# Last product of the output projection: token tiles in the order 0, 2, 1, 3, and the gate multiplied ahead

## The chip, the core and the metric

The kernel runs on one core of a Trainium2 chip. The time is device microseconds of the core, the median over runs. The engines have queues of their own and wait for one another through semaphores: TensorE (PE in the profile; PEld is its weight load), VectorE (DVE), ScalarE (ACT), GpSimd (POOL) and SyncE (SP), which issues nearly all DMAs.

## What is computed

A layer of lightning attention with a routed gate, on x of 4 sequences, 512 tokens each and 512 features, all in float32:

```python
xn = layernorm(x)
s = lightning_attn(xn)        # 16 heads of 128, blocks with decay
g = silu(router_ffn(xn))      # top 8 of 64 experts
out = x + s * g
```

The attention ends in `s = (gate * norm_w * o * rms) @ w_out.T`, where `rms` is one number per token over all 2048 features of `o`. Since it is one number per token, the kernel applies it behind the output projection, together with `g`.

## The kernel before

**Stages.** V projection, then for each pair of sequences (p = 0, 1) the gate, q and k projections with the attention of each head, and at the end the output projection with the router's sum and the final `x + s * g`. Matrix products run as three passes over operands split into a high and a low part (PASSES, lines 27 and 1234): ScalarE writes the high part (line 110), VectorE or GpSimd the low one (line 113).

**Output projection.** For each pair p the product of two sequences with two column halves is made by seven products in place of eight (OUT_PRODUCTS, line 49). Product m runs over 8 groups g of two heads; so there are 112 steps (p, m, g), in the loop of line 1244. A step is 4 token tiles x 3 passes = 12 matmuls of 128x256 (`o_group`, line 1232). Tiles 0 and 1 add up in the two halves of one PSUM accumulator, tiles 2 and 3 in those of another (`acc[t // 2][:, t % 2]`).

**Operands.** `yr` is the left operand of two steps: a load on SP (`load_y`), a cast on ScalarE and a subtraction on VectorE (`split_y`, 128x1024), written into the program five steps ahead (`ahead`, line 1109). Three buffers of it are in use here, so a cast waits until TensorE has done the pair of steps before. `wr` is the right operand of a product, two halves of it, each one cast and two VectorE subtractions of 128x512 (`split_wo`, line 860), written at g = 2 and g = 5 of the product before. Call yr51 the one of steps 102 and 103 (g = 6, 7 of the last pair's sixth product), yr52 to yr55 those of the seventh product's pairs of steps.

**Sums.** After each product `o_sums` (line 890) combines its accumulator with earlier ones that stay in SBUF (`a`, `e`, `c`), and from the fourth product on gives one quarter of the output to `finish` (line 876). For a 128x256 piece that is: VectorE `u = src * rms * u` (L879), where `u` held the gate; GpSimd `u = u + x` (L880); a store from `u`. The stores are issued on SP when the loop comes to g = 3 of the next product (line 1258). In the profile e_o, c_o and a_o are the pieces of the fifth, sixth and seventh product. The second accumulator's sums are written one step into the next product.

**The tail.** In the very last product the last three groups are not run group by group, but tile by tile (TAIL, lines 1287 to 1293): tile t gets its nine matmuls, and then its sums: VectorE `a = acc + a` (L900), `u = a * rms * u` (L879), `u = u + x` (L880, here on VectorE too), and a store, of even tiles on SP and odd ones on ACT (L882).

**Order.** The program's order is each queue's order: the loop writes a step's operands first, then its matmuls, then sums, and nothing is reordered. Every engine takes its instructions in that order.

**Memory.** `decay_row`, 1 KB on each of 16 partitions, holds a table of decays. It is made at the start, and its last reader is a store early in the V projection (`keep_rows`). It lives in the pool of constants, for the whole program. `stage` is a pool that is closed at the end of the V projection; `late` is the pool of the output projection.

Of the kernel before, what the change touches and what calls it, by code (L numbers as in the profile page):

```python
# [8 lines left out]
F32 = mybir.dt.float32  # L9
F32R = mybir.dt.float32r  # L10
AF = mybir.ActivationFunctionType
ALU = mybir.AluOpType
AX = mybir.AxisListType

P = 128
NH = 16
GH = 2
NG = NH // GH
PB = 2
# [41 lines left out]
def kernel(  # L61
# [13 lines left out]
    nc = tc.nc  # L75
# [5 lines left out]
    NT = N // P  # L81
# [6 lines left out]
    def pool(stack, name, bufs=1, **kw):  # L88
        return stack.enter_context(tc.tile_pool(name=name, bufs=bufs, **kw))


    def left(stack, name, bufs=1):
        return pool(stack, name, bufs, side="left", reuse_waits="tile")

    def right(stack, name, bufs=1):
        return pool(stack, name, bufs, side="right", reuse_waits="tile")

    const = pool(ctx, "const")
# [7 lines left out]
    def tok(b, t):  # L106
        return bass.ds(b * N + t * P, P)
# [13 lines left out]
    ones = const.tile([P, 1], F32, tag="ones", name="ones")  # L121
    mhalf = const.tile([P, NT], F32, tag="mhalf", name="mhalf")
    W = 2 * P
    decay_row = const.tile([NH, W], F32, tag="decay_row", name="decay_row")
    by_row = const.tile([P, 2], F32, tag="rest_of", name="rest_of")
    rest_of, slope_of = by_row[:, 0:1], by_row[0:NH, 1:2]
    kdecay = const.tile([P, NH], F32, tag="kdecay", name="kdecay")
# [19 lines left out]
    NM, NQ, H2 = len(PRODUCTS), NG // 2, F // 2  # L147
# [47 lines left out]
    rms = [const.tile([P, NT], F32, tag=f"rms{b}", name=f"rms{b}") for b in range(B)]  # L195
# [25 lines left out]
    def rsqrt(dst, var, scale, eps, name):  # L221
        n = dst.shape[1]
        v = small.tile([P, NT], F32, tag="var", name=f"v_{name}")
        nc.vector.tensor_scalar(v[:, 0:n], var, scale, eps, ALU.mult, ALU.add)
        nc.gpsimd.tensor_tensor(dst, v[:, 0:n], mhalf[:, 0:n], ALU.pow)

    xts = {}
# [328 lines left out]
    def nothing():  # L556
        return [[] for _ in PRODUCTS]
# [7 lines left out]
    def v_weights(p, g, rawp, sump, wp):  # L565
        def loads(raw):
            r = raw.rearrange("p i k (c w) -> p i k c w", c=KC)
            per = VH // GH
            return [
                (r[:, i, k, :, bass.ts(j, GH * P)], w_v[(2 * g + i) * per + j][:, bass.ts(k, KC)])  # L570
                for i in range(2) for k in range(2) for j in range(per)
            ]
        return Weights(f"v_{p}_{g}", KC * VW, rawp, sump, wp, loads, True)
# [209 lines left out]
    def sum_squares(b):  # L783
        ps = ps_sc.tile([P, NT], F32, tag="sc", name=f"ssq_{b}")
        for t in range(NT):
            nc.tensor.matmul(
                ps[:, t : t + 1], sq[b][:, bass.ts(t, P)], ones, start=True, stop=True
            )
        rsqrt(rms[b], ps, 1.0 / (NH * P), RMS_EPS, f"rms{b}")

    gates, ebs = {}, []

    def load_eb(outp):
        ebs.append(outp.tile([P, F], F32, tag="x", name="raw_eb", bufs=PB * NT))
        nc.sync.dma_start(out=ebs[0][0:E, :], in_=expert_b)
        nc.sync.dma_start(out=ebs[0][E : 2 * E, :], in_=expert_b)
# [78 lines left out]

    def finish(b, t, src, j, m, last):
        u, xt, c = gates[b, t], xts[b, t], bass.ts(j, H2)
        tail_ = last and m == NM - 1
        nc.vector.scalar_tensor_tensor(u[:, c], src, rms[b][:, t : t + 1], u[:, c], ALU.mult, ALU.mult)  # L879
        (nc.vector if tail_ else nc.gpsimd).tensor_tensor(u[:, c], u[:, c], xt[:, c], ALU.add)  # L880
        if tail_:
            (nc.scalar if t % 2 else nc.sync).dma_start(out=out[tok(b, t), c], in_=u[:, c])  # L882
        elif last or m > 4:
            d = c if last else slice(0, F)
            stores.append(lambda: nc.sync.dma_start(out=out[tok(b, t), d], in_=u[:, d]))

    ochain = {}


    def o_sums(p, m, x, ps, ts, last):  # L890
        b0 = p * PB
        name = f"o{m}{x}_{p}"

        def temp(n, pool_, tag, bufs=None):
            k = 4 if tag == "sum" else 2
            ochain[n, x] = pool_.tile([P, k, H2], F32, tag=tag, name=f"{n}_{name}", bufs=bufs)[:, 0:2]
            return ochain[n, x]

        def add(dst, what, i=slice(0, 2)):
            nc.vector.tensor_tensor(dst[:, i], ps[:, i], ochain[what, x][:, i], ALU.add)  # L900
        s1 = (wk, "s1", 1) if x == 0 else (late, "s1b", 1) if p or m else (hpools["sum"], "sum", None)
        if m == 0:
            nc.scalar.copy(temp("s1", *s1), ps)
        elif m == 1:
            add(temp("a", wk, "a", 2), "s1")
        elif m == 2:
            add(temp("e", wk, *(("e", 1) if x == 0 else ("sqs", 2))), "a")
        else:

            i2, j2 = ((0, 0), (1, 1), (0, 1), (1, 0))[m - 3]  # L910
            dst = (lambda: ps, lambda: ochain["e", x], lambda: temp("c", *s1), lambda: ochain["a", x])[m - 3]()
            if m > 3:
                add(dst, "e" if m == 4 else "a", slice(ts[0], ts[-1] + 1))
            for i in ts:
                finish(b0 + i2, 2 * x + i, dst[:, i], j2, m, last)
# [60 lines left out]
    stage = right(vs_stack, "stage", 4)  # L976
    rawp, sump = right(vs_stack, "vraw"), right(vs_stack, "vsum")
    vwp, vout = left(vw_stack, "vw", 8), left(vw_stack, "vout", 4)
    ws = [v_weights(0, g, rawp, sump, vwp) for g in range(NV)]
    tiles = [(p, t) for p in range(NP) for t in range(NT)]  # L980
    again = [(p, t) for p in reversed(range(NP)) for t in range(NT)]
# [50 lines left out]
    for k, (p, t) in enumerate(tiles + again):  # L1032
        g, after = k // n1, nothing()
# [106 lines left out]
    for i, (p, kind, n, w) in enumerate(todo):  # L1140
# [19 lines left out]
        if nu - len(XN) + NX <= i < nu:  # L1160
# [3 lines left out]
            m = i - (nu - len(XN) + NX)  # L1164
# [79 lines left out]
    for i, (p, m, g) in enumerate(steps):  # L1244
        last = p == NP - 1
        if i == 6:
            while ysums:
                ysums.pop(0)()

        if i == 16:  # L1250
            ha_stack.close()
            hw_stack.close()
            late = right(late_stack, "late", 2)

        ahead(i, 9 if i == 15 else 10, 5)
        if i == 16:
            load_eb(late)
        while stores and g == 3:
            stores.pop(0)()
        if g == 0:  # L1260
            k, first = OUT_PRODUCTS[m][2:]
            if m < 3:
                q, tag = (ps_sc, "sc") if k == 2 else (ps_mm, "mm")
                if k == 2:
                    spare[:] = [ps_sc.tile([P, F], F32, tag="sc", name=f"spare_{p}")]
                accs[k] = [q.tile([P, 2, H2], F32, tag=tag, name=f"acc{k}{x}_{p}") for x in range(2)]
            acc = accs[k]
        for j, f in ((2, 0), (5, 1)):
            u = i // NG + 1
            if g == j and u in made:  # L1270
                split_wo(made[u], f, win.pop(0))
                nxt = order.index((u, f)) + 2
                if nxt < len(order):
                    win.append(load_wo(made[order[nxt][0]], order[nxt][1]))
        if i == 17:
            split_eb(late)
        for b, t in tiles_at.get(i + 6, ()) if i > 16 else tiles_at[20]:
            if t == 0 and i >= 16:
                load_wT(b, late)

        for b, t in tiles_at[20] if i == 16 else tiles_at.get(i + 5, ()) if i > 16 else ():
            load_x(late, b, t, PB * NT)
        for d, step in ((3, silu_gate), (1, gate_sum), (-1, lambda b, t: center(b, t, late))):
            for b, t in tiles_at.get(i - d, ()):
                step(b, t)
        yr = parts.pop(0)
        if last and m == NM - 1 and g >= NG - TAIL:
            tail.append(yr)
            if g == NG - 1:
                for t in range(NT):  # L1290
                    for n in range(TAIL):
                        o_group(acc, m, NG - TAIL + n, tail[n], t)
                    o_sums(p, m, t // 2, acc[t // 2], (t % 2,), True)
        else:
            for t in range(NT):
                o_group(acc, m, g, yr, t)
            if g == NG - 1:
                for j in range(2):
                    sums.append(lambda p=p, m=m, j=j, a=acc[j], last=last: o_sums(p, m, j, a, (0, 1), last))
                sums.pop(0)()  # L1300

        if sums and (g == 0 or m < 2 or i + 1 < len(steps) and OUT_PRODUCTS[steps[i + 1][1]][2] == k):
            sums.pop(0)()
        if i in (1, 3, 5):
            for f in last_steps[i // 2]:
                f()
        if i in (8, 10):
            sum_squares((b0, b1)[i // 2 - 4])
        for b, t in tiles_at.get(i, ()):
            ffn(b, t)  # L1310
    late_stack.close()
# [44 lines left out]
```

## Time and profile before

| | |
|---|---|
| median of 3 runs | 1057.78 us (1057.56 to 1059.29) |
| profiled execution | 1057.22 us |
| its span, first to last instruction | 1055.4 us |
| matmuls of the output projection, L1235 | 1344, mean 282 ns |
| seventh product of the last pair, first matmul to last | about 1038 to 1051.2 us |

In the profile a line such as `1030.85 1.76 DVE L113 TENSOR_TENSOR yr<-yin,yr 128x1024 fp32r<-128x1024 f32 x1` reads: start and length in us, engine, line of the kernel, operation, what is written from what, the shape of one instruction, and how many stand together. Square brackets at the end hold the engine's idle time before it and what ended that. The waits have three numbers: us in total, how often, and the longest. The view of windows has the stretch, its length, busy time and number of instructions of each engine, and last the granted TensorE clock, the DMA share and GB/s.

### The profile page before, as it was taken

How to read it: one execution, taken by the hardware profiler on the slowest of the kernel's cores; microseconds unless marked ns; L12 is line 12 of the kernel's file. 1: busy time of each engine (PE TensorE's matmuls, PEld its weight loads, DVE VectorE, ACT ScalarE, POOL GpSimd, SP SyncE). 2: the span in 40 equal slices, each digit the busy share in tenths (PEclk: the TensorE clock that was granted, in tenths of full speed). 3: DMA queues.
4: the chain of work that ended last, by engine and by line, in shares of the span. 5: the costliest groups of instructions: out<-in, count | busy, mean ns of one | idle time of the engine just before them, and what ended most of it. 6: DMA issues, size and time to landing. Idle time of an engine off the chain costs nothing.

```text
span 1055.4 us, 17634 instructions
## 1 busy us (share of the span) xinstructions
PE 1042.5 (99%) x6338; PEld 924.5 (88%) x6338; DVE 637.3 (60%) x1017; ACT 553.4 (52%) x969; POOL 680.7 (64%) x698
## 2 busy tenths in 40 slices
PE   9999999999999999999999999999999999999997
PEld 7888888887888878888888888888888889999997
DVE  6666543357677676765554555545555558698767
ACT  5555555554545545455554555545545545574632
POOL 5888781857768776786777778877678753124013
PEclk9999999999999999999999999999999999999999
DMA  7456736544455454553863323533334236989863
GB/s 246 166 203 245 265 141 230 159 125 150 150 150 195 135 170 153 162 183 112 285 225 108 137 66 114 177 109 115 96 108 147 76 135 222 347 299 305 283 220 100
DMA packets 128839, 185.12 MB, mean 175 GB/s; under 512 B 11105, under 2 KB 72689, under 8 KB 127857
## 3 DMA queue, kind: packets, MB, share of 16 engines
q1 hardware_dynamic: 127856, 183.56, 52.7%
q8 instruction: 50, 0.82, 0.3%
q10 hardware_dynamic: 896, 0.44, 0.2%
q14 instruction: 37, 0.29, 0.1%
HBM read 115.26 MB, written 70.80 MB: 176 GB/s over the span
## 4 chain that ended last, share of the span: by engine, by line
PE 91%; DVE 4%; DMA 2%; ACT 1%; issue 1%; POOL 0%; SPq 0%; ACTq 0%; DVEq 0%
PE u_qk L516 27%; PE u_g L516 15%; PE u_v L516 13%; PE acc L1235 12%; PE sa L672 5%; PE o L757 5%; PE ss L695 4%; PE o L759 4%; PE d_v L546 2%; DMA yin<-y 2%; PE kt L675 2%; PE lg L332 1%; PE pt L265 1%; DVE yS L720 1%; DVE wosum L746 1%
## 5 line engine op out<-in xcount | busy, mean ns | idle before, releaser
L1235 PE MATMUL acc<-wr,yr 128*128 128x256 f32 x1344 | 163.4, 282 | 1.3 <-DVE a_o L900 1.3
L1235 PEld LDWEIGHTS acc<-wr,yr 128*128 128x128 f32 x1344 | 161.4, 190 | 3.3 <-DVE a_o L900 1.7
L516 PE MATMUL u_qk<-blk_T,ws_qk 128*128 128x512 f32 x576 | 141.7, 395 | 0.9 <-DVE best L380 0.9
L769 POOL TENSOR_TENSOR sqs<-sqs,sq 128x512 f32<-128x512 f32 x60 | 79.1, 1318 | 94.6 <-ACT sq L768 94.6
L516 PEld LDWEIGHTS u_qk<-blk_T,ws_qk 128*128 128x128 f32 x576 | 106.9, 188 | 23.9 <-issue 1.3
L113 POOL TENSOR_TENSOR ws_qk<-sum_qk,ws_qk 128x512 fp32r<-128x512 f32 x64 | 84.7, 1335 | 29.7 <-ACT ws_qk L110 29.7
L516 PE MATMUL u_qk<-blk_B,wa_qk 128*128 128x512 f32 x384 | 101.7, 400 | 0.0
L880 POOL TENSOR_TENSOR u<-u,x 128x256 f32<-128x256 f32 x28 | 32.4, 1179 | 100.5 <-DVE u L879 70.4
L113 DVE TENSOR_TENSOR yr<-yin,yr 128x1024 fp32r<-128x1024 f32 x56 | 75.3, 1349 | 34.9 <-ACT yr L110 34.8
L560 ACT ACTIVATE k<-k 128x512 f32<-128x512 f32 x64 | 40.5, 632 | 106.2 <-DVE k L507 106.2
L757 PE MATMUL o<-at,vin 128*128 128x128 f32 x512 | 88.5, 275 | 0.0
L110 ACT CAST yr<-yin 128x1024 fp32r<-128x1024 f32 x56 | 58.3, 1046 | 44.7 <-PE acc L1235 36.1
L516 PEld LDWEIGHTS u_qk<-blk_B,wa_qk 128*128 128x128 f32 x384 | 69.8, 189 | 13.6
L761 DVE SCALAR_TENSOR_TENSOR y<-o,nw,gt 128x512 f32<-128x512 f32 x64 | 48.0, 751 | 49.6 <-PE o L759 49.6
L757 PEld LDWEIGHTS o<-at,vin 128*128 128x128 f32 x512 | 74.8, 192 | 2.5
L681 ACT ACTIVATE kd<-kt,kdecay 128x384 f32<-128x384 f32 x64 | 37.2, 581 | 71.8 <-PE kt L675 71.8
L759 PE MATMUL o<-qd,st 128*128 128x128 f32 x384 | 74.3, 275 | 0.0
L768 ACT ACTIVATE sq<-o 128x512 f32<-128x512 f32 x60 | 35.9, 598 | 72.7 <-POOL sqs L769 41.7
L516 PE MATMUL u_g<-blk_T,ws_g 128*128 128x512 f32 x288 | 72.5, 396 | 0.0
L672 PE MATMUL sa<-q,k 128*128 128x128 f32 x512 | 68.0, 276 | 3.2 <-ACT q L560 3.1
L672 PEld LDWEIGHTS sa<-q,k 128*128 128x128 f32 x512 | 64.2, 191 | 7.3 <-ACT q L560 4.8
L699 DVE SCALAR_TENSOR_TENSOR st<-st,bdecay,ss 128x128 f32<-128x128 f32 x128 | 41.7, 346 | 44.2 <-ACT st L697 41.9
(199 smaller groups left out, 2402.3 us busy)
## 6 DMA issues: line engine op xcount, KB each, us to landing
yin<-y SPq DMA_DIRECT2D x56, 512.0 KB, 4.7
v<-vo_v SPq DMA_DIRECT2D x64, 256.0 KB, 2.8
raw_qk<-in_w_head_dram SPq DMA_DIRECT2D x64, 256.0 KB, 4.2
vin<-v SPq DMA_DIRECT2D x64, 256.0 KB, 3.5
y<-yS SPq DMA_DIRECT2D x64, 256.0 KB, 3.4
y<-y SPq DMA_DIRECT2D x48, 256.0 KB, 2.2
woin<-wo SPq DMA_DIRECT2D x18, 512.0 KB, 5.3
x<-in_x_dram SPq DMA_DIRECT2D x32, 256.0 KB, 4.9
```

The source lines that it names most:

```text
L110: nc.scalar.copy(hi, src)
L113: eng.tensor_tensor(lo, src, hi.bitcast(F32), ALU.subtract)
L516: nc.tensor.matmul(ps, lhsT, rhs, start=(first and c == 0 and n == 0), stop=(c == KC - 1 and n == len(PASSES) - 1), skip_group_check=not f ...
L560: nc.scalar.activation(dst, src, AF.Silu)
L672: nc.tensor.matmul(pa[:, c], k[:, c], q[:, c], start=True, stop=True)
L695: nc.tensor.matmul(ps[:, c], kd[s][:, c], v_of(b, h, c), start=True, stop=True)
L699: nc.vector.scalar_tensor_tensor(r[:, c], r[:, c - 1], bdecay[:, h : h + 1], ps[:, c], ALU.mult, ALU.add)
L757: nc.tensor.matmul(o, v_of(b, h, c), at[s][:, c], start=True, stop=(c == 0))
L759: nc.tensor.matmul(o, st[s][:, c - 1], qd[s][:, c - 1], start=False, stop=True)
L761: nc.vector.scalar_tensor_tensor(y, po, nw[:, h : h + 1], gts[s], ALU.mult, ALU.mult)
L769: nc.gpsimd.tensor_tensor(sq[b], sq[b], s1, ALU.add)
L1235: nc.tensor.matmul(acc[t // 2][:, t % 2], yr[:, yi, bass.ts(t, P)], wos[m, g // NQ][:, wi, g % NQ], start=(first and g == 0 and n == 0 and ...
```

## The change

- The tail takes the token tiles in the order 0, 2, 1, 3.
- The last product's piece is out = x + (acc + a) * rms * gate. The part that does not need the last accumulator is made during the sixth product, one tile at the end of each of its steps g = 1 to 4 (`prepare_last`): VectorE multiplies `u` (the gate) by rms; GpSimd makes `ag = a * u` and adds that to x.
- After a tile's last matmul, VectorE then has `u = acc * u` and `u = u + x`, and the store follows on the queue that it had (`finish_last`).
- `ag` is a tile of 1 KB per partition in `late`. `decay_row` goes from the constants to `stage`.
- `finish` loses its branch for the tail.

```diff
-    decay_row = const.tile([NH, W], F32, tag="decay_row", name="decay_row")
...
     def finish(b, t, src, j, m, last):
         u, xt, c = gates[b, t], xts[b, t], bass.ts(j, H2)
-        tail_ = last and m == NM - 1
         nc.vector.scalar_tensor_tensor(u[:, c], src, rms[b][:, t : t + 1], u[:, c], ALU.mult, ALU.mult)
-        (nc.vector if tail_ else nc.gpsimd).tensor_tensor(u[:, c], u[:, c], xt[:, c], ALU.add)
-        if tail_:
-            (nc.scalar if t % 2 else nc.sync).dma_start(out=out[tok(b, t), c], in_=u[:, c])
-        elif last or m > 4:
+        nc.gpsimd.tensor_tensor(u[:, c], u[:, c], xt[:, c], ALU.add)
+        if last or m > 4:
...
+    def prepare_last(b, t, j):
+        u, xt, c = gates[b, t], xts[b, t], bass.ts(j, H2)
+        a = ochain["a", t // 2][:, t % 2]
+        nc.vector.tensor_scalar(u[:, c], u[:, c], rms[b][:, t : t + 1], None, ALU.mult)
+        g = late.tile([P, H2], F32, tag="ag", name=f"ag_{b}_{t}", bufs=1)
+        nc.gpsimd.tensor_tensor(g, a, u[:, c], ALU.mult)
+        nc.gpsimd.tensor_tensor(xt[:, c], xt[:, c], g, ALU.add)
+
+    def finish_last(b, t, ps, j):
+        u, xt, c = gates[b, t], xts[b, t], bass.ts(j, H2)
+        nc.vector.tensor_tensor(u[:, c], ps[:, t % 2], u[:, c], ALU.mult)
+        nc.vector.tensor_tensor(u[:, c], u[:, c], xt[:, c], ALU.add)
+        (nc.scalar if t % 2 else nc.sync).dma_start(out=out[tok(b, t), c], in_=u[:, c])
...
+    decay_row = stage.tile([NH, W], F32, tag="decay_row", name="decay_row", bufs=1)
...
-                for t in range(NT):
+                for t in sorted(range(NT), key=lambda t: t % 2):
                     for n in range(TAIL):
                         o_group(acc, m, NG - TAIL + n, tail[n], t)
-                    o_sums(p, m, t // 2, acc[t // 2], (t % 2,), True)
+                    finish_last(p * PB + 1, t, acc[t // 2], 0)
...
+        if last and m == NM - 2 and 1 <= g <= NT:
+            prepare_last(p * PB + 1, g - 1, 0)
```

## The prediction

> **What bounds the kernel now.** I read the page first, then the chain, the waits of the last 30 us, and the timelines of VectorE (DVE), GpSimd (POOL) and TensorE (PE) there.
>
> ```profile
> PE 1042.5 (99%) x6338; PEld 924.5 (88%) x6338; DVE 637.3 (60%) x1017; ACT 553.4 (52%) x969; POOL 680.7 (64%) x698
> ...
> 1046.67 1.36 PE acc L1235 x9
> 1048.03 0.02 issue
> 1048.05 0.43 DVE a_o L900
> ...
> 1049.85 1.35 PE acc L1235 x9
> 1051.20 0.02 issue
> 1051.22 0.43 DVE a_o L900
> ```
>
> First line, the page: matmuls bound the program. The rest is the end of the chain of waits: matmuls of one token tile alternate with VectorE's work, and nothing else is on the path.
>
> ```profile
> PEld acc L1235 <- DVE a_o L900: 1.7, 2, 1.0
> PE acc L1235 <- DVE a_o L900: 1.3, 2, 0.8
> ```
>
> The waits from 1026 us on: in the tail TensorE waits twice for VectorE, 0.52 + 0.76 us. Tiles 0 and 1 share one accumulator, 2 and 3 the other; before tile 1 (and 3) starts, the add of its neighbour must have read that accumulator.
>
> ```profile
> 1030.85 1.76 DVE L113 TENSOR_TENSOR yr<-yin,yr 128x1024 fp32r<-128x1024 f32 x1
> 1032.53 1.83 DVE L113 TENSOR_TENSOR wr<-woin,wr 128x512 fp32r<-128x512 f32 x2
> 1034.28 1.22 DVE L113 TENSOR_TENSOR yr<-yin,yr 128x1024 fp32r<-128x1024 f32 x1
> 1035.42 1.28 DVE L113 TENSOR_TENSOR wr<-woin,wr 128x512 fp32r<-128x512 f32 x2
> 1036.62 1.22 DVE L113 TENSOR_TENSOR yr<-yin,yr 128x1024 fp32r<-128x1024 f32 x1
> 1037.76 0.68 DVE L900 TENSOR_TENSOR c_o<-acc,a_o 128x512 f32<-128x512 f32 x1
> 1038.47 0.88 DVE L879 SCALAR_TENSOR_TENSOR u<-c_o,rms,u 128x256 f32<-128x256 f32 x2
> 1039.27 1.76 DVE L113 TENSOR_TENSOR yr<-yin,yr 128x1024 fp32r<-128x1024 f32 x1
> 1040.96 0.68 DVE L900 TENSOR_TENSOR c_o<-acc,a_o 128x512 f32<-128x512 f32 x1
> 1041.67 0.88 DVE L879 SCALAR_TENSOR_TENSOR u<-c_o,rms,u 128x256 f32<-128x256 f32 x2
> 1042.47 1.77 DVE L113 TENSOR_TENSOR yr<-yin,yr 128x1024 fp32r<-128x1024 f32 x1
> ```
>
> VectorE's timeline (start, length), through the stretch into which the change puts work. Its mean share of 60% misleads here: from 1030.85 to 1044.24 it has no gap. Each yr line makes the operand of two steps of TensorE.
>
> ```profile
> 1030.75 2.46 POOL L880 TENSOR_TENSOR u<-u,x 128x256 f32<-128x256 f32 x2 [0.50 <-DVE u L879]
> 1039.04 2.59 POOL L880 TENSOR_TENSOR u<-u,x 128x256 f32<-128x256 f32 x2 [5.83 <-DVE u L879]
> 1042.23 2.60 POOL L880 TENSOR_TENSOR u<-u,x 128x256 f32<-128x256 f32 x2 [0.60 <-DVE u L879]
> ```
>
> GpSimd's timeline. Laid beside the last view, it shows what matters most: a yr takes 1.76 or 1.77 us where a POOL add runs and 1.22 where none does, and two wr take 1.83 against 1.28. So a VectorE instruction with both inputs in SBUF is held up 0.54 us by one POOL instruction, and POOL's next one waits for VectorE in turn (two adds take 2.46 to 2.60 us here, two free ones 1.43 at 1015.32): they alternate. An e_o add of L900, with one input in PSUM, keeps its 0.68 us beside a POOL add at 1028.87.
>
> **The change, part by part.**
>
> *Order 0, 2, 1, 3.* Neighbouring turns now use different accumulators, so both waits go. From tile 0's last matmul (1046.15) to tile 3's (1051.19) is 5.04 us now. The matmuls run at 16.41 us for 137 where nothing stops them, 0.12 each; 27 take 3.2. Gain 1.8 (the two waits and the restarts). Next late: nothing, since tile 0's result is read some 0.4 us after its matmuls and tile 1 starts 1.1 us after them.
>
> *One instruction less after the last matmul.* Add 0.42, scale 0.48, add 0.42 run from 1051.19 to 1052.63, 1.44 us. The new pair is two tensor_tensor of that size: 0.42 + 0.42 and two handovers of 0.04, 0.92. Gain 0.5. The stores keep their sizes, engines and parity (even tiles on SP, odd on ACT). Their spacing shrinks to some 1.1 us; issue takes 0.35 and landing 1.7 (page, ACT queue), so I price this at nothing, at most 0.3. SP's two last stores stand behind the four stores of c_o, which will be late, but all POOL adds end before tile 0 is done (below).
>
> *Four multiplies by rms on VectorE* (steps 1 to 4 of product six, 128x256, one input). No such row exists. Below: COPY 128x256 at its fastest, 0.29; above: the two-input scalar_tensor_tensor, 0.48. TENSOR_SCALAR at twice the size has 0.54. I take 0.35: the copy plus the 0.06 by which a scalar operand lengthens that size (0.48 against 0.42). The next instruction starts 0.08 before a record ends (1035.42 against 1034.28 + 1.22), so 0.27 each, 1.1 in all. Ends 0.8 and 1.6.
>
> *Eight POOL instructions* (product a times gate, then added to x), in POOL's queue behind the e_o adds that end at 1033.21 and ahead of c_o's. The cover for POOL itself is its idle 5.83 us before 1039.04; free, eight need 5.7. But they hold up VectorE: by the alternation, every instruction with SBUF inputs from the first multiply on meets one. Walking both queues: the last e_o adds stand ahead of multiply 0 and yr51 (the yr of steps 6, 7); the eight then fall before wr, wr, yr52, multiply 3, wr, wr, yr53, and beside the c_o add, which does not mind. Seven times 0.54 is 3.8. Ends: zero if POOL always fits beside; 4.3 if all eight hold.
>
> *VectorE's sum:* 1.1 + 3.8 = 4.9 us late. Who waits: ACT releases show when TensorE frees a pair of steps (1038.00, 1040.88; 2.85 apart), so the last product needs yr52 at 1037.98, yr53 at 1040.83, yr54 at 1043.68, and yr55 at 1045.46, three matmuls into the tail. They are ready now at 1035.50, 1037.84, 1041.03 and 1044.24. The walk, by ends: multiply 0 1031.8, e_o add 1032.3, yr51 1033.5, POOL 1034.0, wr 1034.7, POOL 1035.2, wr 1035.8, multiplies 1 and 2 1036.3, POOL 1036.9, yr52 1038.1, POOL 1038.6, multiply 3 1038.9, POOL 1039.4, wr 1040.0, POOL 1040.6, wr 1041.2, POOL 1041.7, yr53 1042.9; then c_o's add, two scales and a held yr take 3.2 us as now, twice: yr54 1046.1, yr55 1049.3. TensorE stops 0.1, 2.0, 0.3 and 1.7 us; behind the last stop it stands 3.9 us late, which is 4.9 (the walk says 5.0) less yr55's slack of 1.2, with 0.2 for semaphore and matmul restart. c_o's adds end at about 1049.9, tile 0 at 1050.1, so nothing else is late.
>
> *decay_row moved from the constants to the staging pool, a 1 KB tile ag in its place.* Same instructions, same queues. Its last reader, the store of rows, is issued early in the V projection, and ag's place was freed tens of us earlier. Price nothing; a shift of addresses could move tile reuse by some tenths either way, as TensorE has only 7 us of gaps in all, the longest 1.5.
>
> *Sum:* +3.9 - 1.8 - 0.5 = **+1.6 us**. The profiled execution is 1057.22 us (span 1055.4 and 1.8 around it), so 1058.8; the median of the runs is 0.56 higher: **1059.4**. The ends move it so: a multiply of 0.29 or 0.48 by -0.2 or +0.5; a handover of 0.41 (the TENSOR_SCALAR row at twice the size, median 0.95 against 0.54) in place of 0.54 by -1.6, with the later stops; an eighth one by +0.5; landing by +0.3; addresses by 0.3 either way. Hardly all at once: -0.2 to +3.0.
>
> *Clock.* The granted clock in the stretch after the last matmul reads:
>
> ```profile
> 1052.75:1055.40 2.65, 0.00 (x0) 0.00 (x0) 0.00 (x0) 0.00 (x0) 0.00 (x0) 0.50 0.15 49
> ```
>
> (the last three are clock, DMA share, GB/s). It is at half 1.5 us after TensorE's last matmul at 1051.19. The forecast's stops of 2.0 and 1.7 us are that long, so a drop is not excluded. Half clock on the tail's 33 remaining matmuls would add up to 3.9 us; after the earlier stop it would mostly be swallowed by the next. The Trainium skill, "TensorE: Matmul & The Clock Gate", section "Why this matters for your kernels", says that only gaps over about 3 us drop the clock; by it the price is zero. The row is stricter than that sentence, but stands in an execution's end. I take zero for the sum, since the windows from 249 to 254 and from 383 to 388 us, with gaps of TensorE of 1.5 and 1.2 us in them, read 1.00, and keep 3.9 as the end.
>
> **Rivals.**
>
> *The cover holds* (faster): VectorE's lateness stays under yr55's slack of 1.2 us plus what the tail saves. For it: before 1026 VectorE has gaps of 1.6 us per pair, and POOL is idle. Against it: VectorE has no gap where the work lands. If handovers cost nothing and only the 1.1 us of multiplies count, the gain is 1.8 + 0.5 = 2.3: 1055.5. Between this and the forecast the sign turns where VectorE is 3.3 us late.
>
> *Half clock after the stop at yr55* (slower): place and price above, it needs a drop within 1.8 us of idling. +1.6 + 1.7 to 3.9, about +4: 1061.8.
>
> *Multiplies wait too* (slower): should a multiply wait until the store or add of the other half of the same gate tile is over, VectorE's queue, with yr51 and yr52 behind it, stops for the store's 2.1 us. Against it: block tiles are written part by part while matmuls read other parts, without gaps. +1.5 to +2: 1061.
>
> **How the numbers follow.** Forecast 0.62, cover holds 0.14, half clock 0.18, waiting multiplies 0.06. A measurement of this kernel tells about 0.2%, 2.1 us, from no change. The forecast's own range, -0.2 to +3.0 around +1.6, passes 2.1 in somewhat over a third: 0.40 same and 0.22 slower. The cover gives 0.12 faster and 0.02 same; half clock and waiting multiplies 0.24 slower. Faster 0.12, same 0.42, slower 0.46. The range runs from 1056.2 to 1061.9; below lie most cases of a held cover, above the worse half of the clock's.
>
> **What would show it.** Right: yr of the last product at 1.7 us each, wr at 1.2; TensorE idle before yr53 and yr55, by some 2 us each; no wait on an accumulator in the tail; 0.9 us of VectorE after the last matmul; POOL busy without gap from 1030 to 1046. Wrong: yr at 1.22 us beside POOL's products, or TensorE without gaps until its last matmul: then the cover held. A granted clock below 1.00 in the last 10 us speaks for the second rival, a multiply behind a DMA for the third.

## The result and the profile after

The changed kernel takes 1060.81 us (median of 12 runs, 1059.34 to 1063.27), the one before on the same chip 1058.06 (1057.06 to 1059.74): a ratio of 1.0020, 95% interval 1.0011 to 1.0029, so 1.2 to 3.1 us slower (the two medians are 2.75 us apart). On a second chip it was 1.0014 (1.0005 to 1.0023). The forecast was +1.6 us, a ratio of 1.0015, and a range of 1056.2 to 1061.9 us.

The page of the changed kernel first, then two of its waits from 1026 us on, ScalarE's for TensorE and TensorE's for VectorE (us in total, times, longest us):

```profile
PE 1043.0 (99%) x6338; PEld 924.8 (87%) x6338; DVE 640.0 (60%) x1017; ACT 553.5 (52%) x969; POOL 690.5 (65%) x706
```

```profile
ACT yr L110 <- PE acc L1246: 8.9, 6, 1.8
...
PE acc L1246 <- DVE yr L113: 3.0, 3, 1.2
```

The page's shares hardly differ; GpSimd has 9.8 us more. The waits do: the two on a shared accumulator are gone, and three on the operand yr have come, 3.0 us in place of 1.3. The timeline of VectorE shows why, beside the lines shown of the kernel before. Line numbers have moved: L889 is the new multiply by rms, L891 and L892 GpSimd's product and add, L896 and L897 the tail's two instructions, L877, L878 and L910 what was L879, L880 and L900, and L1246 the matmuls.

```profile
1028.77 1.23 DVE L113 TENSOR_TENSOR yr<-yin,yr 128x1024 fp32r<-128x1024 f32 x1
...
1031.89 0.83 DVE L889 TENSOR_SCALAR u<-u,rms 128x256 f32<-128x256 f32 x1
1032.64 1.75 DVE L113 TENSOR_TENSOR yr<-yin,yr 128x1024 fp32r<-128x1024 f32 x1
1034.32 2.37 DVE L113 TENSOR_TENSOR wr<-woin,wr 128x512 fp32r<-128x512 f32 x2
1036.61 0.60 DVE L889 TENSOR_SCALAR u<-u,rms 128x256 f32<-128x256 f32 x2
1037.14 1.21 DVE L113 TENSOR_TENSOR yr<-yin,yr 128x1024 fp32r<-128x1024 f32 x1
1038.27 0.83 DVE L889 TENSOR_SCALAR u<-u,rms 128x256 f32<-128x256 f32 x1
1039.02 1.83 DVE L113 TENSOR_TENSOR wr<-woin,wr 128x512 fp32r<-128x512 f32 x2
1040.77 1.76 DVE L113 TENSOR_TENSOR yr<-yin,yr 128x1024 fp32r<-128x1024 f32 x1
1042.45 0.68 DVE L910 TENSOR_TENSOR c_o<-acc,a_o 128x512 f32<-128x512 f32 x1
1043.17 1.94 DVE L877 SCALAR_TENSOR_TENSOR u<-c_o,rms,u 128x256 f32<-128x256 f32 x2
1045.03 1.75 DVE L113 TENSOR_TENSOR yr<-yin,yr 128x1024 fp32r<-128x1024 f32 x1
...
1048.21 1.76 DVE L113 TENSOR_TENSOR yr<-yin,yr 128x1024 fp32r<-128x1024 f32 x1
...
1054.21 0.43 DVE L896 TENSOR_TENSOR u<-acc,u 128x256 f32<-128x256 f32 x1 [0.26 <-PE acc L1246]
1054.74 0.42 DVE L897 TENSOR_TENSOR u<-u,x 128x256 f32<-128x256 f32 x1
```

Two wr now take 2.37 us in the first pair and 1.83 in the second, where they took 1.83 and 1.28, and the c_o scales 1.94 instead of 0.88. A free multiply takes 0.34 us, one behind a GpSimd instruction 0.83. TensorE's timeline has the three stops:

```profile
1042.58 3.01 PE L1246 MATMUL acc<-wr,yr 128*128 128x256 f32 x24 [0.58 <-DVE yr L113]
1046.83 1.99 PE L1246 MATMUL acc<-wr,yr 128*128 128x256 f32 x15 [1.24 <-DVE yr L113]
1050.03 4.08 PE L1246 MATMUL acc<-wr,yr 128*128 128x256 f32 x32 [1.20 <-DVE yr L113]
```

From the last line on there is no pause: the rest of the tail's 4 tiles runs through.

The spans differ by 2.6 us (1055.4 and 1058.0), and not all of that is the change's. At 912 us TensorE waited once for the expert biases, which it did not before:

```profile
PE pu L820 <- POOL ebs L113: 0.9, 1, 0.9
```

So I compare a stretch behind that: from the start of yr50 (the operand of g = 4, 5 of the sixth product) to the end of the last VectorE instruction. It is 1027.72 to 1052.63, **24.9 us**, before, and 1028.77 to 1055.16, **26.4 us**, after. Behind it both spans last 2.8 us more. The change costs 1.5 us there. Its two ends in the kernel before are:

```profile
1027.72 1.23 DVE L113 TENSOR_TENSOR yr<-yin,yr 128x1024 fp32r<-128x1024 f32 x1
...
1052.20 0.42 DVE L880 TENSOR_TENSOR u<-u,x 128x256 f32<-128x256 f32 x1
```

### The profile page after: what moved, and what is told of

Same layout as the page of the kernel before. It is cut to its first block, busy times and chain, and to the rows that moved or that the text cites. A ratio compares the mean times of both kernels' runs of the same rounds, so it can differ in the third digit from the quotient of the medians.

```text
span 1058.0 us, 17651 instructions
## 1 busy us (share of the span) xinstructions
PE 1043.0 (99%) x6338; PEld 924.8 (87%) x6338; DVE 640.0 (60%) x1017; ACT 553.5 (52%) x969; POOL 690.5 (65%) x706
## 4 chain that ended last, share of the span: by engine, by line
PE 89%; DVE 6%; DMA 2%; ACT 1%; issue 1%; SPq 0%; POOL 0%; ACTq 0%; DVEq 0%
PE u_qk L515 27%; PE u_g L515 15%; PE u_v L515 13%; PE acc L1246 10%; PE sa L671 5%; PE o L756 5%; PE ss L694 4%; PE o L758 4%; PE d_v L545 2%; PE kt L674 2%; DVE yr L113 1%; PE lg L331 1%; DMA yin<-y 1%; ACT yr L110 1%; DVE wr L113 1%
## 5 line engine op out<-in xcount | busy, mean ns | idle before, releaser
L1246 PE MATMUL acc<-wr,yr 128*128 128x256 f32 x1344 | 163.6, 282 | 3.0 <-DVE yr L113 3.0
L1246 PEld LDWEIGHTS acc<-wr,yr 128*128 128x128 f32 x1344 | 161.4, 190 | 5.2 <-DVE yr L113 3.8
L515 PEld LDWEIGHTS u_qk<-blk_T,ws_qk 128*128 128x128 f32 x576 | 106.9, 188 | 23.8 <-issue 1.3
L878 POOL TENSOR_TENSOR u<-u,x 128x256 f32<-128x256 f32 x28 | 31.5, 1144 | 94.5 <-DVE u L877 78.9
```

Source lines behind the costliest of these rows:

```text
L515: nc.tensor.matmul(ps, lhsT, rhs, start=(first and c == 0 and n == 0), stop=(c == KC - 1 and n == len(PASSES) - 1), skip_group_check=not f ...
L1246: nc.tensor.matmul(acc[t // 2][:, t % 2], yr[:, yi, bass.ts(t, P)], wos[m, g // NQ][:, wi, g % NQ], start=(first and g == 0 and n == 0 and ...
```

## The experiments

Ratios are against the kernel before on the same chip, with 95% intervals. "The stretch" is the one above.

**The tile order alone (e1_order)**

```diff
-                for t in range(NT):
+                for t in sorted(range(NT), key=lambda t: t % 2):
```

> The kernel before with nothing but the tile order 0, 2, 1, 3 in the tail; the three VectorE instructions per tile stay. Theory (the waits on the shared accumulator, 0.52 + 0.76 us and the restarts behind them, are all that the order removes): both waits are gone from the profile, from tile 0's last matmul to tile 3's is 3.2 us instead of 5.04, and the time is 1.8 us below before. Rival (matmuls that follow without a pause meet another limit, such as VectorE's reads of the other accumulator): the matmuls of the tail take more than 0.12 us each and the gain is under 0.8 us.

Measured: 0.9980 (0.9972 to 0.9989). TensorE has no pause to its last matmul:

```profile
1029.80 21.52 PE L1235 MATMUL acc<-wr,yr 128*128 128x256 f32 x180
```

Its end, counted from yr50's start (1029.67 here), is 21.65 us away against 23.47 before: 1.8 us gained, as expected. But the stretch is 23.8 us, a gain of only 1.1; the runs, with 1.2 to 3.0, put it somewhat higher. The rest is in VectorE's timeline:

```profile
1049.46 0.42 DVE L900 TENSOR_TENSOR a_o<-acc,a_o 128x256 f32<-128x256 f32 x1
1049.92 0.48 DVE L879 SCALAR_TENSOR_TENSOR u<-a_o,rms,u 128x256 f32<-128x256 f32 x1
1050.43 0.43 DVE L880 TENSOR_TENSOR u<-u,x 128x256 f32<-128x256 f32 x1
1050.78 0.42 DVE L900 TENSOR_TENSOR a_o<-acc,a_o 128x256 f32<-128x256 f32 x1
```

A tile's three instructions take 1.32 us from start to start, its nine matmuls 1.08. So VectorE falls behind over the four tiles and ends 2.2 us after TensorE, where it was 1.4. To gain its full 1.8 us, the order needs the instruction less.

**The move of decay_row alone (e3_move)**

```diff
-    decay_row = const.tile([NH, W], F32, tag="decay_row", name="decay_row")
...
+    decay_row = stage.tile([NH, W], F32, tag="decay_row", name="decay_row", bufs=1)
```

> The kernel before with nothing but decay_row moved from the constants to the staging pool. Theory (the changed kernel's late start of the router's matmuls at 912 us, a wait of 0.91 us for the low part of the expert biases, is a DMA that landed late in that one execution): the time is that of before within 0.3 us, and the wait at 912 us is 0 to 0.9, without relation to the move. Rival (the shift of addresses changes which transfers wait): a wait of some 0.9 us at 912 us here too, and the time 1 us above before.

Measured: 1.000 (0.999 to 1.001), the stretch 24.9 us, and no wait at 912 us at all. The move costs nothing in the stretch, and in the runs nothing over 1 us. Nor is the wait its doing: e1_order, which lacks the move, waits 0.9 us there, and this run, which has it, does not.

**The changed kernel again (e7_again)**

> The changed kernel once more, for a second profile. Theory (the wait at 912 us is of one execution; the change itself costs 1.6 us): three stops of TensorE in the last product of 0.6, 1.2 and 1.2 us again, but at 912 us a wait other than 0.91, and 1.6 us over before. Rival (the wait belongs to the program): 0.91 us again at 912 us, and 2.6 over before.

Measured: 1.0014 (1.0005 to 1.0023). The stretch is 26.4 us to the hundredth, with stops of 0.58, 1.16 and 1.20. At 912 us there were two waits, 0.56 and 0.91, so 1.5 us in all. Neither my theory (another wait than 0.91) nor the rival (0.91 alone) has it exactly; what it shows is that this wait changes between executions of one program, while the stretch does not.

**The new order undone (e2_prepare)**

```diff
-                for t in sorted(range(NT), key=lambda t: t % 2):
+                for t in range(NT):
```

> The changed kernel with the old tile order 0, 1, 2, 3; the multiplies and products stay in the sixth product. From yr50's start to the end of the last VectorE instruction it is 24.9 us before and 26.4 in the changed kernel. Theory: the stops before yr53 to yr55 cost 3.5, the instruction less saves 0.5 and shortens the second wait on an accumulator by 0.3, so 27.6 in that stretch, and 2.7 us over before. Rival (the order hides nothing, since TensorE is late anyway): as the changed kernel, 26.4.

Measured: 1.0024 (1.0011 to 1.0036), the stretch 28.1 us, 0.5 more than I expected, in part because the two waits on an accumulator shrank by hardly 0.1 us in all, not by 0.3. Both kinds of stop stand together:

```profile
PE acc L1246 <- DVE yr L113: 3.0, 3, 1.2
PE acc L1246 <- DVE u L896: 1.2, 2, 0.6
```

In the changed kernel the order thus saves 1.7 us (28.1 to 26.4). It is the preparation that loses more than that.

**Without GpSimd's eight (e5_no_products)**

```diff
-        g = late.tile([P, H2], F32, tag="ag", name=f"ag_{b}_{t}", bufs=1)
-        nc.gpsimd.tensor_tensor(g, a, u[:, c], ALU.mult)
-        nc.gpsimd.tensor_tensor(xt[:, c], xt[:, c], g, ALU.add)
```

> The changed kernel without GpSimd's eight products and adds: the last quarter of the output lacks a times gate times rms. Theory (seven handovers of 0.54 us make VectorE late, the four multiplies' 1.1 us are under yr55's slack of 1.2): no stop of TensorE in the last product, 22.6 us from yr50 to the end against 24.9 before, time 2.3 us below before. Rival (the multiplies in VectorE's queue are what is late): stops of TensorE of 1 us or more, no faster than before.

Measured: 0.9975 (0.9962 to 0.9988), the stretch 22.6 us; TensorE has no wait after 1030 us. VectorE's lines, multiplies in place:

```profile
1035.00 1.28 DVE L113 TENSOR_TENSOR wr<-woin,wr 128x512 fp32r<-128x512 f32 x2
1036.21 0.60 DVE L889 TENSOR_SCALAR u<-u,rms 128x256 f32<-128x256 f32 x2
1036.73 1.21 DVE L113 TENSOR_TENSOR yr<-yin,yr 128x1024 fp32r<-128x1024 f32 x1
1037.87 0.34 DVE L889 TENSOR_SCALAR u<-u,rms 128x256 f32<-128x256 f32 x1
1038.13 1.28 DVE L113 TENSOR_TENSOR wr<-woin,wr 128x512 fp32r<-128x512 f32 x2
```

All at their free lengths. (Ahead of them the first multiply, 0.83, and yr51, 1.75, are held by the e_o adds, which the kernel before has too.) The multiplies alone are hidden by yr55's slack; the lateness that counts comes from GpSimd.

**Without VectorE's four (e6_no_multiply)**

```diff
-        nc.vector.tensor_scalar(u[:, c], u[:, c], rms[b][:, t : t + 1], None, ALU.mult)
```

> The changed kernel without VectorE's four multiplies by rms, GpSimd's eight instructions as they are: the last quarter of the output is not multiplied by rms. Theory: VectorE is still late by eight handovers, so TensorE stops before yr54 and yr55 by some 3 us in all; 25.6 us from yr50 to the end, time 0.7 us over before. Rival (the multiplies are what is late): as without products, 22.6 us and 2.3 below before.

Measured: 0.9999 (0.9987 to 1.0010), the stretch 25.5 us, two stops of 1.1 and 1.2 us, 2.3 in all where I expected some 3. The time expected, +0.7 us, is inside the interval, and the stretch is 0.6 over before. VectorE's lines there:

```profile
1034.34 2.38 DVE L113 TENSOR_TENSOR wr<-woin,wr 128x512 fp32r<-128x512 f32 x2
1036.64 1.76 DVE L113 TENSOR_TENSOR yr<-yin,yr 128x1024 fp32r<-128x1024 f32 x1
1038.32 2.37 DVE L113 TENSOR_TENSOR wr<-woin,wr 128x512 fp32r<-128x512 f32 x2
1040.62 1.76 DVE L113 TENSOR_TENSOR yr<-yin,yr 128x1024 fp32r<-128x1024 f32 x1
```

Every line is held. So the two runs tell the causes apart: products without multiplies stop TensorE, multiplies without products do not. On top of the products the multiplies are not free: without them the stretch is 25.5 us, with them 26.4.

**The eight on VectorE itself (e8_vector)**

```diff
-        nc.gpsimd.tensor_tensor(g, a, u[:, c], ALU.mult)
-        nc.gpsimd.tensor_tensor(xt[:, c], xt[:, c], g, ALU.add)
+        nc.vector.tensor_tensor(g, a, u[:, c], ALU.mult)
+        nc.vector.tensor_tensor(xt[:, c], xt[:, c], g, ALU.add)
```

> The changed kernel with the eight products and adds on VectorE too, in the place where GpSimd's are issued. Theory (GpSimd's instruction costs VectorE 0.54 us by the handover, its own of the same size 0.35): VectorE is 3.8 us late in place of 4.9, 25.5 us from yr50 to the end, time 0.6 us over before and 1 below the changed kernel. Rival (GpSimd takes the work off VectorE): VectorE gets later than in the changed kernel, 27 us or more.

Measured: 1.0006 (0.9996 to 1.0016), the stretch 26.1 us. It is no worse than on GpSimd, and 0.3 us shorter in the stretch, but I had expected 25.5 there, 0.6 too little. The three instructions of a tile:

```profile
1036.99 0.35 DVE L889 TENSOR_SCALAR u<-u,rms 128x256 f32<-128x256 f32 x1
1037.37 0.42 DVE L891 TENSOR_TENSOR ag<-a_o,u 128x256 f32<-128x256 f32 x1
1037.83 0.42 DVE L892 TENSOR_TENSOR x<-x,ag 128x256 f32<-128x256 f32 x1
1038.17 1.22 DVE L113 TENSOR_TENSOR yr<-yin,yr 128x1024 fp32r<-128x1024 f32 x1
```

They take 1.18 us, not 0.96: each needs the result of the one before, and so starts some 0.04 after its end instead of 0.08 ahead of it. From yr50's start to yr55's end it is 21.0 us, so VectorE is 4.5 us late, and 4.7 in the changed kernel: work moved to an idle GpSimd cost VectorE as much as doing the work itself.

**Prepared two products earlier (e4_early, e10_early_again)**

```diff
-        if last and m == NM - 2 and 1 <= g <= NT:
+        if last and m == NM - 4 and 1 <= g <= NT:
```

> The changed kernel with the same multiplies and products written into the fourth product of the last pair, steps 1 to 4, in place of the sixth. There VectorE has gaps of 1.0 to 1.6 us per pair of steps and GpSimd is idle. Theory (the cost is VectorE's lateness in a stretch without a gap, not the instructions as such): no stop of TensorE before yr53 and yr55, tail without waits, time 2.3 us below before (1.8 from the order, 0.5 from the instruction less) and some 4 below the changed kernel. Rival (the handovers cost wherever they stand, or the lateness carries on to the end): between before and the changed kernel, TensorE still waits in the last product.

> The kernel with the multiplies and products in the fourth product once more, on the same chip as the one with the earlier load. Theory: 2.3 to 2.9 us below before, 22.7 us from yr50 to the end of the last VectorE instruction. Rival (its first result was a lucky chip): less than 1.5 us below before.

Measured: 0.9974 (0.9964 to 0.9983), 1055.84 us against 1058.76, and on another chip 0.9978 (0.9964 to 0.9993). The stretch is 22.7 us both times, 2.2 below before and 3.7 below the changed kernel. The second chip's interval, 0.7 to 3.8 us below before, does not by itself exclude the rival of under 1.5; the stretch, the same on both chips, does. TensorE's timeline of e4_early has one line to the end. VectorE's timeline of that place in the kernel before, and then of e4_early:

```profile
1019.72 31.35 PE L1246 MATMUL acc<-wr,yr 128*128 128x256 f32 x263
```

```profile
1013.48 1.23 DVE L113 TENSOR_TENSOR yr<-yin,yr 128x1024 fp32r<-128x1024 f32 x1 [1.60 <-ACT yr L110]
```

```profile
1009.53 1.23 DVE L113 TENSOR_TENSOR yr<-yin,yr 128x1024 fp32r<-128x1024 f32 x1 [0.77 <-ACT yr L110]
1010.67 1.09 DVE L889 TENSOR_SCALAR u<-u,rms 128x256 f32<-128x256 f32 x2
1012.35 1.23 DVE L113 TENSOR_TENSOR yr<-yin,yr 128x1024 fp32r<-128x1024 f32 x1 [0.59 <-ACT yr L110]
```

VectorE still waits for ScalarE's casts there, 0.77 and 0.59 us where it waited 1.60; the added work is taken from that waiting. This kernel beats both the one before and the changed one with the same instructions in another place.

**The biases' load one place earlier (e9_biases)**, on top of e4_early:

```diff
-        ahead(i, 9 if i == 15 else 10, 5)
         if i == 16:
             load_eb(late)
+        ahead(i, 9 if i == 15 else 10, 5)
```

> The kernel with the multiplies and products in the fourth product, and the load of the expert biases issued one step's loads earlier on SP (two lines exchanged). The wait of TensorE for the biases at 912 us was 0, 0.9 or 1.5 us from one execution to another, whichever the kernel. Theory (the load stands behind a 512 KB load in the queue and lands just in time): it lands 0.5 us or more earlier, the wait is 0 to 0.9, and the time 0.5 us below the one with the early products. Rival (the landing is set by the DMA engines' load): the wait stays as it is, and the time too.

Measured: 0.9965 (0.9952 to 0.9978) against 0.9978 (0.9964 to 0.9993) of e10_early_again on the same chip. The intervals overlap by most of their width, and only times were compared; whether the load lands earlier stays open.

## Why the prediction was right

*The order, -1.8.* Right for TensorE: in e1_order its last matmul comes 1.8 us earlier. As a term by itself it was too large, since alone it shortens the stretch by 1.1: I had looked for something late next only at the first tile, and VectorE's three instructions, 1.32 us against 1.08 of matmuls, fall behind only over the tiles after it. With two instructions per tile the term holds: in e4_early the last matmul comes 1.8 us earlier. In the changed kernel it gave 1.7: from the first matmul that needs yr55 to the last matmul it is 4.07 us, where it was 5.73.

*One instruction less, -0.5.* Measured 0.4: from TensorE's last matmul, 1054.10, to VectorE's end, 1055.16, is 1.06 us, not 0.92. Each of the two instructions started 0.1 us after what it waited for; I had taken 0.04. In e5_no_products, without GpSimd's eight, they start after 0.02 and 0.04 us, and 0.90 us is all they take. In the changed kernel the chain has a semaphore instruction of VectorE's queue (DVEq) ahead of each of the two, which it lacks in e5_no_products:

```profile
1054.14 0.02 DVEq L896
...
1054.21 0.44 DVE u L896
```

*VectorE 4.9 us late.* Measured 4.7: from yr50's start to yr55's end is 16.5 us before (1027.72 to 1044.23) and 21.2 after (1028.77 to 1049.97). The multiply is 0.34 (taken 0.35), and there were seven handovers more than before, of 0.47 to 0.57. Their places I had wrong. GpSimd's second product waited for its multiply:

```profile
1037.10 1.85 POOL L891 TENSOR_TENSOR ag<-a_o,u 128x256 f32<-128x256 f32 x1 [0.96 <-DVE u L889]
...
1043.20 0.74 POOL L891 TENSOR_TENSOR ag<-a_o,u 128x256 f32<-128x256 f32 x1
1044.02 0.80 POOL L892 TENSOR_TENSOR x<-x,ag 128x256 f32<-128x256 f32 x1
```

It therefore came too late for yr52, which passed in 1.21 us, one wr later passed freely too, and the last product and add fell on the two c_o scales (1.94 us) instead of beside the c_o add. That the count came to seven all the same was luck: two places that I had named fell out, and two that I had not came in. So the stops were 0.6, 1.2 and 1.2 before yr53, yr54 and yr55, where I had 0.1, 2.0, 0.3 and 1.7 from yr52 on. (Those four add up to 4.1, not to the 3.9 that I used; the walk's own times give 1.4 for the last one and 3.8 in all. The releases that I read as 2.85 us apart are 2.88 apart, which moves the walk by less than 0.1.) Their effect at the tail agrees: the matmuls behind yr55 start at 1050.03. Against 1045.46 before, plus the 1.0 by which this execution was late at yr50, that is 3.5 us, where I had 3.9.

*decay_row, 0.* Right as far as e3_move can tell: nothing in the stretch.

*The sum, +1.6.* In the stretch +1.5, twice: 3.5 - 1.7 - 0.4 with the terms as measured, to within rounding. The mechanism was right; that the sum came so close is in part luck, since three terms were each too large, the cost by 0.4 and the two gains by 0.1 each. In runs 1.0020 and 1.0014; the first median is 1.4 us over the predicted 1059.4, inside the range.

*The rivals.* "The cover holds" is what happens without the eight (e5_no_products) or with all of it two products earlier; its price of -2.3 was right (-2.3 and -2.2 in the stretch), but not its place. "Multiplies wait too" did not occur: no multiply waited longer than one handover (0.83 us). "Half clock" did not occur either; the view of windows of the changed kernel over the three stops, and then over the tail's matmuls, has clock 1.00 (third number from the end):

```profile
1041.00:1051.00 10.00, 6.98 (x56) 6.38 (x55) 8.91 (x10) 1.05 (x1) 8.72 (x8) 1.00 0.12 39
1050.00:1054.00 4.00, 3.97 (x32) 3.87 (x32) 2.55 (x6) 0.00 (x0) 0.56 (x1) 1.00 0.26 86
```

The longest stop was 1.24 us, not 2.0, so it did not test the 1.5 us that I had feared.

## What to carry to other kernels

An idle engine is not free room when its instructions hold up the busy one. Before moving work onto GpSimd, look whether VectorE has gaps in that very stretch, and count up to one handover per moved instruction (seven for eight here, some 0.5 us each). Ask also who consumes what VectorE makes there and with how much slack, since here 1.0 us of lateness cost nothing (e5_no_products) and 4.7 cost 3.5. If work can be done early, put it where the engine it disturbs waits anyway: two products earlier the same instructions turned +1.5 us into -2.2.

## What the runs showed of the hardware

- The clock's fall at the end is not tied to a fixed idle time. Before, it was at half 1.5 us after the last matmul, in the changed kernel 2.7 us after; in e10_early_again, whose last matmul ends at 1050.29, it still stood at full 3.8 us later:

```profile
1050.30:1054.10 3.80, 0.00 (x0) 0.00 (x0) 0.85 (x2) 0.00 (x0) 0.00 (x0) 1.00 0.25 84
```

The Trainium skill, "TensorE: Matmul & The Clock Gate", section "Why this matters for your kernels", advises against idle gaps over about 3 us between bursts of matmuls. Both gaps here stand behind the last matmul; the 1.5 us of the first profile is under that figure, the 3.8 us here is over it and passed at full clock. The trace's own record of the clock tells more: its entry at full lasts 1047.89 us in the kernel before, 1051.31 us in the changed kernel and in e10_early_again, and 1054.72 us in e7_again, which is 307, 308 and 309 times 3.4133 us. So in these traces the fall came a whole number of such steps after that entry began, wherever the last matmul stood in the step.

- TensorE's wait for the expert biases at 912 us was 0 before and in e3_move and e8_vector, 0.4 to 1.5 us in the other profiles, also in two of one program (0.91, and 0.56 + 0.91). It blurs a comparison of whole spans by as much as this change moves; a stretch that starts behind it repeated to 0.01 us.
